# Banks, transposes and sums of a GRU gate in a fused two-layer graph network: p_n in another PSUM pool, transposes moved forward, GpSimd's sums reordered

## The chip, the cores and the metric

The kernel runs on one core of a Trainium2 chip. The metric is device time in microseconds, from the first to the last instruction. The engines are named as the profile names them: PE (TensorE, matmuls) with PEld (its weight loads), DVE (VectorE), ACT (ScalarE), POOL (GpSimd) and SP (SyncE, which here only issues DMAs).

## What is computed

The input is 64 graphs of 256 nodes with 256 features each, and a 256x256 adjacency for each. Everything is float32. Layer 0 is a normalised graph convolution with a residual and a layernorm. Layer 1 has two branches over its input x: a convolution branch along the nodes (a 1x1 convolution, ReLU, a 17-tap convolution, both with batch norm) and a message branch (a Gaussian similarity times the mask, times messages). A GRU cell joins them:

```python
x_conv = transpose(relu(h + xc))          # h: the 17-tap convolution, xc: x transposed
x_in = concatenate([x_conv, x_nmp], axis=-1)
gi = x_in @ w_ih.T + b_ih
gh = x @ w_hh.T + b_hh
r = sigmoid(gi_r + gh_r)
z = sigmoid(gi_z + gh_z)
nn_ = tanh(gi_n + r * gh_n)
x_gru = (1.0 - z) * nn_ + z * x
out = layernorm(x + x_gru)
```

## The kernel before, in words

The 64 graphs are worked in four quarters of 16 (`Q = 16`). The 17-tap convolution is done in a transformed domain, for a whole quarter at once, and so a quarter passes through stages:

- `layer0` and `layer1` of each graph (a graph's layers leave x transposed and the message branch in DRAM as `xn_d`, the layer 0 output as `x1_d`, and their transformed part in `V`);
- `products`, 12 steps of matmuls p_k with streamed weights;
- `real_transform`, `complex_begin` and `complex_end`, the inverse transform: VectorE work on the large tile `VM` (also called `M`), with no matmuls, whose `output` writes the convolution of the quarter to DRAM (`xc_d`);
- `gates`, one GRU cell (`gru`) for each graph.

Stages of different quarters are woven into each other with Python generators: each `yield` ends a piece, `merge(a, b, n)` takes a piece of b after every n of a, `take(s, n)` gives the next n pieces. The first four gates of a quarter run with the layers of the next quarter. The other twelve are `late`: 48 pieces, of which 14 go between the steps of the next quarter's `products`, and the rest are merged with `complex_end` (`end`) and, where there is a next quarter, with its first layers (`begin`). After the last quarter nothing is left to merge, so its 16 gates run alone. What stands in the code is a priority: the framework lays out each engine's instructions at build time, by that order and by what it expects to be ready. In the trace, L816 of a gate runs before L798, which stands ahead of it in the code. At run time each engine takes its instructions in the order laid out, and waits on semaphores.

There are two PSUM pools of four 128x512 tiles each. `bank` gives one of the pool `ps`, used by the layers and by the transposes p_xcT. `accbank` gives one of `psacc`, used by `products` (p_k) and by the gates (p_rz, p_n).

One gate, `gru(g)`, goes like this. It starts the loads for graph g + 1 (`load_gate`, L708 and L710). The sums r and z take 21 matmuls of 128x128 by 128x256 instead of 24, by a Strassen-like scheme over halves of the inputs; for this, GpSimd computes four sums of input halves beforehand (`input_sums`, L737 to L740, into one buffer `sums`). Each fp32 matmul is two instructions. The first twelve of the 21 (L756) fill two tiles p_rz; VectorE reads them at L769 and L770. The other nine fill two more, read at L775 and L776. ScalarE then takes two tanh (L778, L780). In the same piece come the transposes for the next graph, `transposed(g + 1)`: 4 transposes on TensorE (p_xcT, L726), and two relus on ScalarE (L728), which write the last third of the next `inputs`. Then, for each half of the nodes, 6 matmuls p_n (L793), read at L798, followed by a chain on VectorE, a tanh (L805), and after the second half the blend with x, the layernorm (with a power on GpSimd, L293, between two VectorE instructions, L292 and L301) and the output DMA.

The transposes need `xc_g`: the convolution's output loaded by `load_conv` (L704), to which `residual` (L715) adds x1 by an accumulating DMA issued by GpSimd.

Of the kernel before, what the change touches and what calls it, by code (L numbers as in the profile page):

```python
# [11 lines left out]
ALU = mybir.AluOpType  # L12
# [14 lines left out]
def kernel(  # L27
# [27 lines left out]
    nc = tc.nc  # L55
# [10 lines left out]
    Q = P // GT  # L66
# [16 lines left out]
    def accbank(name):  # L83
        return psacc.tile([P, 512], F32, tag="acc", name=name)
# [613 lines left out]


    GATE, CONV, SUMS = {}, {}, {}  # L700

    def load_conv(g):
        CONV[g] = gate.tile([P, NCH, D], F32, name="xc_g")
        nc.sync.dma_start(CONV[g], xc_d[g // Q][g % Q].rearrange("(c p) d -> p c d", p=P))  # L704
# [8 lines left out]
    def residual(g):  # L713

        nc.gpsimd.dma_start(  # L715
            CONV[g], x1_d[g // Q][g % Q].rearrange("(c p) d -> p c d", p=P), accum_op=ALU.add
        )

    def transposed(g):

        xc = CONV.pop(g)
        xcT = GATE[g][1][:, 2 * DCH :]
        p = bank("p_xcT").rearrange("p (k n) -> p k n", k=DCH)
        for k in range(DCH):
            for c in range(NCH):
                nc.tensor.transpose(p[:, k, c * P : (c + 1) * P], xc[:, c, k * P : (k + 1) * P], ident)  # L726
        for k in range(DCH):
            nc.scalar.activation(xcT[:, k], p[:, k], AF.Relu, bias=bn2_bias[:, k : k + 1])  # L728
# [5 lines left out]
    def input_sums(g):  # L734
        A11, A12, A21, A22 = halves(GATE[g][1])
        S = SUMS[g] = gate.tile([P, 4, HALF, P], F32, name="sums", bufs=1)
        nc.gpsimd.tensor_tensor(S[:, 2], A11, A21, op=ALU.subtract)  # L737
        nc.gpsimd.tensor_tensor(S[:, 0], A21, A22, op=ALU.add)  # L738
        nc.gpsimd.tensor_tensor(S[:, 1], S[:, 0], A11, op=ALU.subtract)  # L739
        nc.gpsimd.tensor_tensor(S[:, 3], A12, S[:, 1], op=ALU.subtract)  # L740

    def gru(g):

        following = g % Q + 1 < Q
        (x1, inputs), S = GATE.pop(g), SUMS.pop(g)
        trz = gate.tile([P, 4, D], F32, name="trz", bufs=1)
        nn = gate.tile([P, NCH, D], F32, name="nn", bufs=1)
        if following:  # L750
            load_gate(g + 1)
        A11, A12, A21, A22 = halves(inputs)

        def block(p, j, a, b):
            for k in range(HALF):
                nc.tensor.matmul(  # L756
                    p[:, j * D : (j + 1) * D], a[:, k], wrz[:, b, k], start=k == 0, stop=k == HALF - 1
                )

        p15, p26 = accbank("p_rz"), accbank("p_rz")  # L760
        block(p15, 0, A11, B11)
        block(p26, 0, A12, B21)
        block(p15, 1, S[:, 0], T1)
        block(p26, 1, S[:, 1], T2)
        yield
        if following:
            residual(g + 1)
        first = gate.tile([P, 2, D], F32, name="first", tag="gn")
        nc.vector.tensor_add(first, half(p15), brz_t)  # L769
        nc.vector.tensor_add(trz[:, 0:2], first[:, 0:1].to_broadcast([P, 2, D]), half(p26))  # L770
        p7, p34 = accbank("p_rz"), accbank("p_rz")
        block(p7, 0, S[:, 2], T3)
        block(p34, 0, S[:, 3], B22)
        block(p34, 1, A22, T4)
        nc.vector.tensor_add(trz[:, 3], trz[:, 1], p7[:, :D])  # L775
        nc.vector.tensor_add(trz[:, 1:3], trz[:, 1:4:2], half(p34))  # L776

        nc.scalar.activation(trz[:, 0:4:2], trz[:, 0:4:2], AF.Tanh, scale=0.5)  # L778
        nc.vector.tensor_add(trz[:, 1:4:2], trz[:, 1:4:2], first[:, 1:2].to_broadcast([P, 2, D]))
        nc.scalar.activation(trz[:, 1:4:2], trz[:, 1:4:2], AF.Tanh, scale=0.5)  # L780
        if following:
            transposed(g + 1)
        yield
        for c in range(NCH):
            terms = [(inputs[:, k, c * P : (c + 1) * P], wn[:, k]) for k in range(3 * DCH)]
            if c == 0 and following:
                input_sums(g + 1)
            if c == 1 and g % Q + 2 < Q:
                load_conv(g + 2)
            p = accbank("p_n")  # L790
            for o, part in ((1, terms[:DCH]), (0, terms[DCH:])):
                for j, (lhsT, w) in enumerate(part):
                    nc.tensor.matmul(  # L793
                        p[:, o * D : (o + 1) * D], lhsT, w, start=j == 0, stop=j == len(part) - 1
                    )

            gn = gate.tile([P, 2, D], F32, name="gn")
            nc.vector.tensor_add(gn, p.rearrange("p (i d) -> p i d", i=2), bn_t)  # L798
            nc.vector.scalar_tensor_tensor(
                gn[:, 1, :], trz[:, 2 * c], 1.0, gn[:, 1, :], op0=ALU.add, op1=ALU.mult  # L800
            )
            nc.vector.scalar_tensor_tensor(  # L802
                gn[:, 0, :], gn[:, 1, :], 0.5, gn[:, 0, :], op0=ALU.mult, op1=ALU.add
            )
            nc.scalar.activation(nn[:, c, :], gn[:, 0, :], AF.Tanh)  # L805


            if g == B - 1:
                part = slice(c, c + 1)
            elif c == NCH - 1:  # L810
                part = slice(0, NCH)
            else:
                yield
                continue
            y, t, n = x1[:, part], trz[:, 1:4:2][:, part], nn[:, part]
            nc.vector.scalar_tensor_tensor(y, t, 3.0, y, op0=ALU.add, op1=ALU.mult)  # L816
            nc.vector.scalar_tensor_tensor(n, t, 1.0, n, op0=ALU.subtract, op1=ALU.mult)
            nc.vector.tensor_sub(y, y, n)
            layernorm(y, nc.scalar, 4 * LN_EPS)
            nc.scalar.dma_start(out[g].rearrange("(c p) d -> p c d", p=P)[:, part], y)  # L820
            yield


    def merge(main, other, every=1):

        for i, _ in enumerate(main):
            yield
            if i % every == every - 1 and next(other, "end") != "end":
                yield
        yield from other  # L830

    def chain(*stages):
        for stage in stages:
            yield from stage
# [13 lines left out]
    def run(stage):  # L848
        for _ in stage:
            pass  # L850
# [69 lines left out]
    def gates(q, part):  # L920

        for i in part:
            if i == 0:
                load_conv(q * Q)
                load_gate(q * Q)
                yield
                load_conv(q * Q + 1)
                residual(q * Q)
                yield
                transposed(q * Q)  # L930
                yield
                input_sums(q * Q)
                yield
            yield from gru(q * Q + i)
# [5 lines left out]
    for q in range(NQ):  # L940
        first = (q + 1) * Q
        more = q + 1 < NQ
        end = complex_end(q)
        if more:
            if q:
                others = [both(take(late, 3 if i % 3 == 0 else 2), take(end, 2)) for i in range(AHEAD)]
            else:
                others = [nothing() for _ in range(AHEAD)]
            begin = chain(merge(layer0(first), layer0(first + 1)), graphs(first, range(AHEAD), V2, others))
        sums(0)  # L950
        real = real_transform()
        for step in range(STEPS):
            if step < 4:
                run(products(step))
            else:
                run(merge(products(step), take(real, 1)))
                run(complex_begin(step))
            if q:
                run(take(late, (0, 1, 1, 1, 1, 1, 2, 1, 2, 1, 2, 1)[step]))
            else:  # L960
                run(take(begin, 2 + step // 4))
        run(real)
        if not q:
            run(merge(begin, end, 3))
        elif more:
            run(merge(merge(take(late, 20), take(begin, 6), 3), take(end, 5), 5))
            run(begin)
        else:
            run(merge(late, end, 2))
        if more:  # L970
            run(late)
            run(end)
            for f in range(0, FL, 12):
                nc.scalar.copy(V[:, f : f + 12, :, : AHEAD * GT], V2[:, f : f + 12])
            early = gates(q, range(EARLY))
            others = [take(early, 2) for _ in range(Q)]
            run(graphs(first, range(AHEAD, Q), V, others))
            run(early)
            late = gates(q, range(EARLY, Q))
        else:  # L980
            run(gates(q, range(Q)))
# [53 lines left out]
```

## Time and profile before

The median of 3 runs is 2213.34 us (2213.03 to 2220.08). The profiled execution has a span of 2214.4 us, with 29080 instructions.

| Engine | Busy, us | Share of the span |
|---|---|---|
| PE | 2077.4 | 94% |
| PEld | 1753.5 | 79% |
| DVE | 1564.9 | 71% |
| ACT | 835.9 | 38% |
| POOL | 670.2 | 30% |

The chain that ended last is PE for 50% of the span, DVE for 13% and POOL for 5%. In that chain the gate's matmuls stand first, L756 with 18% and L793 with 9%; the three lines L738, L739 and L740 of the sums have 1% each.

How to read the lines that follow: in a group, "busy, mean ns" is followed by the idle time of the engine just before these instructions and by what ended most of it, with the line of the releaser. The idle time of a group is time in which the whole engine stood still. A line of a table of windows gives, for each engine, its busy microseconds in the stretch and the number of instructions; the last three columns are the TensorE clock granted, the share of the DMA engines, and GB/s. In the list of waits, the numbers are the total in us, the number of times and the longest. In the 40 slices of the page a slice is 2214.4 / 40 = 55.4 us long.

### The profile page before, as it was taken

To read this page: it belongs to the slowest core of one execution; us is meant where nothing else is said; L and a number is where in the kernel's file an instruction comes from. 1 tells how busy PE (TensorE), PEld (TensorE's weight loads), DVE (VectorE), ACT (ScalarE), POOL (GpSimd) and SP (SyncE) were. 2 spreads that over 40 slices of the span, in tenths; PEclk is the share of its full clock that TensorE was granted. 3 is DMA by queue.
4 is the path that set the end of the run, shared out by engine and by line. 5 is a ranking of instruction groups with operands and counts; after the bars stand their busy time and mean duration, and the time that the engine had idled before them with its cause. 6 is when DMAs were issued, how large, how long until landed. Compare 5 with 4: busy or idle time off the path is not lost.

```text
span 2214.4 us, 29080 instructions
## 1 busy us (share of the span) xinstructions
PE 2077.4 (94%) x9853; PEld 1753.5 (79%) x9853; DVE 1564.9 (71%) x3749; ACT 835.9 (38%) x1850; POOL 670.2 (30%) x653
## 2 busy tenths in 40 slices
PE   5999989969999998999999998899999999889998
PEld 4777767848888886788888887688888887678887
DVE  6655448794657899855556989955555879987666
ACT  3555533435441122446543122445554112222222
POOL 2333331113231233322322233321331123344442
PEclk9999999989999999999999999999999999999999
DMA  3655467544337644424334754433323754444342
GB/s 108 193 166 169 150 193 258 170 134 115 118 92 214 200 138 116 132 86 124 105 106 148 214 160 125 143 96 105 119 87 113 216 171 114 115 120 113 102 110 57
DMA packets 251424, 305.20 MB, mean 138 GB/s; under 512 B 18602, under 2 KB 230074, under 8 KB 251275
## 3 DMA queue, kind: packets, MB, share of 16 engines
q1 hardware_dynamic: 183180, 199.85, 29.2%
q10 hardware_dynamic: 45280, 68.04, 8.7%
q0 software_dynamic: 22816, 35.45, 8.1%
q8 instruction: 78, 1.28, 0.2%
q14 instruction: 70, 0.57, 0.1%
HBM read 200.71 MB, written 102.57 MB: 137 GB/s over the span
## 4 chain that ended last, share of the span: by engine, by line
PE 50%; DVE 13%; issue 6%; POOL 5%; ACT 4%; DMA 0%; ACTq 0%; POOLq 0%; SPq 0%; DVEq 0%
PE p_rz L756 18%; PE p_n L793 9%; PE p_k L486 8%; PE p_nmp L462 3%; PE p_out L368 2%; PE p_dft L431 2%; PE p_conv L396 2%; PE p_hT L358 2%; PE p_msg L417 1%; POOL sums L738 1%; POOL ln_rs L293 1%; PE p_dist L455 1%; POOL sums L740 1%; POOL sums L739 1%; DVE gn L798 1%
## 5 line engine op out<-in xcount | busy, mean ns | idle before, releaser
L756 PE MATMUL p_rz<-wrz,sums 128*128 128x256 f32 x1536 | 356.0, 383 | 19.5 <-DVE gn L798 9.8
L793 PE MATMUL p_n<-wn,inputs 128*128 128x256 f32 x1536 | 351.3, 381 | 16.3 <-DVE first L769 15.7
L756 PEld LDWEIGHTS p_rz<-wrz,sums 128*128 128x128 f32 x1536 | 288.6, 191 | 70.9 <-issue 15.8
L793 PEld LDWEIGHTS p_n<-wn,inputs 128*128 128x128 f32 x1536 | 285.7, 190 | 62.2 <-DVE first L769 18.9
L756 PE MATMUL p_rz<-wrz,inputs 128*128 128x256 f32 x1152 | 272.8, 380 | 2.1 <-ACT inputs L728 1.5
L293 POOL TENSOR_TENSOR ln_rs<-ln_rs,neg_half 128x2 f32<-128x2 f32 x129 | 100.4, 778 | 541.3 <-DVE ln_rs L292 455.7
L756 PEld LDWEIGHTS p_rz<-wrz,inputs 128*128 128x128 f32 x1152 | 216.8, 190 | 33.7 <-ACT inputs L728 3.6
L805 ACT ACTIVATE nn<-gn 128x256 f32<-128x256 f32 x128 | 53.2, 416 | 325.6 <-DVE gn L802 324.8
L486 PE MATMUL p_k<-u,VM 128*128 128x256 f32 x736 | 175.1, 380 | 0.8 <-DMA u<-ud 0.8
L329 POOL TENSOR_TENSOR dis<-deg,neg_half 128x2 f32<-128x2 f32 x64 | 49.9, 780 | 403.5 <-DVE deg L327 324.9
L303 ACT ACTIVATE x_g<-x_g,ln_mr,ln_rs 128x256 f32<-128x256 f32 x128 | 70.0, 593 | 256.1 <-DVE ln_mr L301 256.1
L486 PEld LDWEIGHTS p_k<-u,VM 128*128 128x128 f32 x736 | 138.3, 190 | 21.2 <-DMA u<-ud 2.2
L431 PE MATMUL p_dft<-fwd,h 128*128 128x240 f32 x512 | 118.2, 375 | 27.2 <-ACT h L400 27.2
L737 POOL TENSOR_TENSOR sums<-inputs 128x384 f32<-128x384 f32 x64 | 70.0, 1093 | 241.6 <-issue 172.0
L396 PE MATMUL p_conv<-wc,xn 128*128 128x259 f32 x512 | 128.1, 393 | 12.2 <-ACT xn L388 12.2
L358 PE MATMUL p_hT<-adjT,x 128*128 128x256 f32 x512 | 126.8, 392 | 10.0 <-DVE adjT L341 9.3
L431 PEld LDWEIGHTS p_dft<-fwd,h 128*128 128x128 f32 x512 | 95.9, 192 | 44.0 <-ACT h L400 36.4
L462 PE MATMUL p_nmp<-aT,msg 128*128 128x256 f32 x512 | 125.5, 389 | 5.0 <-DVE aT L457 5.0
L368 PE MATMUL p_out<-w,hT 128*128 128x256 f32 x512 | 124.4, 386 | 1.3 <-ACT hT L363 1.1
L396 PEld LDWEIGHTS p_conv<-wc,xn 128*128 128x128 f32 x512 | 98.0, 194 | 31.5 <-ACT xn L388 16.4
L351 POOL TENSOR_TENSOR x_t<-x_t,b_t 128x512 f32<-128x512 f32 x64 | 85.2, 1332 | 121.9 <-ACT x L350 93.2
L417 PE MATMUL p_msg<-wmsg,xn 128*128 128x256 f32 x512 | 122.0, 381 | 0.0
(153 smaller groups left out, 3880.0 us busy)
## 6 DMA issues: line engine op xcount, KB each, us to landing
u<-ud SPq DMA_DIRECT2D x284, 256.0 KB
xn_d<-xn ACTq DMA_DIRECT2D x64, 512.0 KB
inputs<-xn_d SPq DMA_DIRECT2D x64, 512.0 KB
adj_t<-in_adj_dram SPq DMA_DIRECT2D x64, 256.0 KB
x_t<-in_x_dram SPq DMA_DIRECT2D x64, 256.0 KB
x_d<-x ACTq DMA_DIRECT2D x64, 256.0 KB
x_g<-x_d SPq DMA_DIRECT2D x64, 256.0 KB
xc_d<-VM SPq DMA_DIRECT2D x64, 256.0 KB
```

The lines of the kernel that those rows point to most:

```text
L293: nc.gpsimd.tensor_tensor(rs[:, : len(chunks)], rs[:, : len(chunks)], neg_half[:, : len(chunks)], op=ALU.pow)
L303: nc.scalar.activation(y[:, c, :], y[:, c, :], AF.Identity, bias=mr[:, c : c + 1], scale=rs[:, c : c + 1])
L351: nc.gpsimd.tensor_tensor(x_t, x_t, b0_t.unsqueeze(1).to_broadcast([P, NCH, D]), op=ALU.add)
L358: nc.tensor.matmul(p[:, k, :], x1[:, mc, k * P : (k + 1) * P], adjT[:, mc, 1 - mc : 3 - mc, :].rearrange("p n q -> p (n q)"), start=mc == ...
L368: nc.tensor.matmul(p[:, c, :], hT[:, k, c * P : (c + 1) * P], w0[:, k, :], start=k == 0, stop=k == DCH - 1)
L396: nc.tensor.matmul(p, x1T[:, k, c * P : (c + 1) * P], wc1[:, k, :], start=k == 0, stop=k == DCH - 1)
L417: nc.tensor.matmul(p[:, c, :], x1T[:, k, c * P : (c + 1) * P], wmsg[:, k, :], start=k == 0, stop=k == DCH - 1)
L431: nc.tensor.matmul(p[:, t0 * FL : t1 * FL], h[:, c, k * P : (k + 1) * P], fwd[:, first : first + t1 - t0, :].rearrange("p t f -> p (t f)") ...
L462: nc.tensor.matmul(p[:, k, :], msg[:, mc, k * P : (k + 1) * P], aT[:, mc].rearrange("p n q -> p (n q)"), start=mc == 0, stop=mc == NCH - 1,)
L486: nc.tensor.matmul(p[:, j * D : (j + 1) * D], v[:, k, :], u[:, k, :], start=k == 0, stop=k == DCH - 1)
L756: nc.tensor.matmul(p[:, j * D : (j + 1) * D], a[:, k], wrz[:, b, k], start=k == 0, stop=k == HALF - 1)
L793: nc.tensor.matmul(p[:, o * D : (o + 1) * D], lhsT, w, start=j == 0, stop=j == len(part) - 1)
```

## The change

It has four parts, which keep all arithmetic as it was.

1. A flag `ALONE` is set before each quarter's `products`, from the second quarter on, and cleared where the next quarter's remaining layers begin. While it is set, the two p_n tiles of a gate come from the pool `ps` instead of `psacc`. This is meant to use the layers' banks where no layers run. (In the merged stage with `begin`, a few pieces of layers do run while it is set.)
2. `transposed(g + 1)` moves from the end of the gate's second piece to the end of the first, behind the first twelve of the 21 matmuls, and so on ScalarE ahead of the gate's two tanh.
3. For this the loads come earlier: `load_conv(g + 2)` moves from the second half of p_n to the first piece, and `residual` runs one graph further ahead: `residual(g + 2)` in the second half of p_n instead of `residual(g + 1)` after the first piece. `gates` starts the second graph's residual itself.
4. GpSimd computes the four sums in the order in which the matmuls use them: S[:, 2] comes third instead of first.

```diff
     def input_sums(g):
...
-        nc.gpsimd.tensor_tensor(S[:, 2], A11, A21, op=ALU.subtract)
         nc.gpsimd.tensor_tensor(S[:, 0], A21, A22, op=ALU.add)
         nc.gpsimd.tensor_tensor(S[:, 1], S[:, 0], A11, op=ALU.subtract)
+        nc.gpsimd.tensor_tensor(S[:, 2], A11, A21, op=ALU.subtract)
         nc.gpsimd.tensor_tensor(S[:, 3], A12, S[:, 1], op=ALU.subtract)
...
         block(p26, 1, S[:, 1], T2)
-        yield
         if following:
-            residual(g + 1)
+            transposed(g + 1)
+        if g % Q + 2 < Q:
+            load_conv(g + 2)
+        yield
...
         nc.scalar.activation(trz[:, 1:4:2], trz[:, 1:4:2], AF.Tanh, scale=0.5)
-        if following:
-            transposed(g + 1)
         yield
...
             if c == 1 and g % Q + 2 < Q:
-                load_conv(g + 2)
-            p = accbank("p_n")
+                residual(g + 2)
+            p = (bank if ALONE[0] else accbank)("p_n")
...
                 transposed(q * Q)
+                residual(q * Q + 1)
                 yield
...
+        ALONE[0] = q > 0
         sums(0)
...
             run(merge(merge(take(late, 20), take(begin, 6), 3), take(end, 5), 5))
+            ALONE[0] = False
             run(begin)
```

More of the change, by code (lines that the diff above doesn't have):

```diff
@@ L700 @@
     GATE, CONV, SUMS = {}, {}, {}
+    ALONE = [False]
     def load_conv(g):
@@ L764, in gru @@
         block(p26, 1, S[:, 1], T2)
+        if following:
+            transposed(g + 1)
+        if g % Q + 2 < Q:
+            load_conv(g + 2)
         yield
-        if following:
-            residual(g + 1)
         first = gate.tile([P, 2, D], F32, name="first", tag="gn")
@@ L780, in gru @@
         nc.scalar.activation(trz[:, 1:4:2], trz[:, 1:4:2], AF.Tanh, scale=0.5)
-        if following:
-            transposed(g + 1)
         yield
```

## The prediction

> **What bounds the kernel now.** I read the page first (share of each engine, the slices, the chain of waits), then the groups of the gate's matmuls, then a table of windows by stage, then who waited for whom in the one long stretch where TensorE has gaps, and last the chain in order of time where that stretch ends. The page:
>
> ```profile
> PE 2077.4 (94%) x9853; PEld 1753.5 (79%) x9853; DVE 1564.9 (71%) x3749; ACT 835.9 (38%) x1850; POOL 670.2 (30%) x653
> ...
> PE   5999989969999998999999998899999999889998
> ...
> DVE  6655448794657899855556989955555879987666
> ...
> L756 PE MATMUL p_rz<-wrz,sums 128*128 128x256 f32 x1536 | 356.0, 383 | 19.5 <-DVE gn L798 9.8
> L793 PE MATMUL p_n<-wn,inputs 128*128 128x256 f32 x1536 | 351.3, 381 | 16.3 <-DVE first L769 15.7
> ...
> L756 PE MATMUL p_rz<-wrz,inputs 128*128 128x256 f32 x1152 | 272.8, 380 | 2.1 <-ACT inputs L728 1.5
> ```
>
> TensorE is the engine in demand, but not evenly: it dips in three places, and there VectorE stands at 8 to 9 tenths. In front of the gate's matmuls TensorE sat idle 19.5 + 16.3 + 2.1 = 37.9 us, nearly all for VectorE reading a PSUM bank (L798, L769) or for GpSimd's sums. The table of windows gives busy time by stage (columns: PE, PEld, DVE, ACT, POOL with counts, granted clock, DMA share, GB/s):
>
> ```profile
> 700.00:780.00 80.00, 80.00 (x376) 70.42 (x376) 68.25 (x134) 13.70 (x28) 17.72 (x15) 1.00 0.68 204
> 800.00:900.00 100.00, 85.66 (x383) 71.38 (x381) 97.57 (x223) 27.86 (x59) 40.26 (x34) 0.95 0.43 121
> ...
> 1320.00:1420.00 100.00, 84.34 (x383) 69.58 (x382) 97.57 (x223) 28.41 (x60) 39.96 (x34) 0.97 0.43 121
> ...
> 1820.00:1955.00 135.00, 119.41 (x549) 100.24 (x548) 131.37 (x270) 29.77 (x60) 49.89 (x44) 1.00 0.38 108
> 1955.00:1975.00 20.00, 17.39 (x78) 13.67 (x77) 16.05 (x29) 4.75 (x10) 9.12 (x9) 1.00 0.60 167
> 1975.00:2200.00 225.00, 225.00 (x1073) 198.13 (x1072) 158.24 (x309) 58.12 (x122) 94.55 (x91) 1.00 0.39 101
> ```
>
> While `products` runs (700 to 780) and in the 15 last gates (1975 to 2200) TensorE has no gap at all: nothing is to be had there. All of TensorE's gaps in gates lie in the three stretches where the gates of the quarter before run against `complex_end`, and in those VectorE is busy 97.57 of 100, 97.57 of 100 and 131.37 of 135 us. **So the gate's PSUM waits are mostly a symptom: VectorE is the bound there.** The list of waits from 1820 to 1975 shows which ones:
>
> ```profile
> PE p_n L793 <- DVE first L769: 7.2, 8, 1.3
> ...
> PE p_rz L756 <- DVE gn L798: 6.7, 7, 1.3
> ...
> PE p_rz L756 <- POOL sums L738: 2.9, 4, 1.6
> ```
>
> And the chain of waits in order of time at the hand-over from this stretch to the last gates (g = 48 is the first that needs the `complex_end` just finished):
>
> ```profile
> 1953.72 3.02 DMA xc_d<-VM
> ...
> 1957.78 3.83 DMA xc_g<-xc_d
> ...
> 1973.08 6.86 PE p_rz L756 x30
> ```
>
> **What the Trainium skill says.** "PSUM — Partial Sum Buffer", Specifications: eight banks of 2 KiB a partition, and Terms: a matmul's output stays within one. The two pools hold four 128x512 fp32 tiles each, all eight; moving p_n takes a bank from the layers' four, it makes none. The trace agrees only indirectly (p_n waits for L769, which frees a bank). "GPSIMD Engine Reference", Key points: GpSimd shares its SBUF interfaces with VectorE and they contend when VectorE has two SBUF inputs. The trace agrees: L301 has a mean of 842 ns from 1820 to 1955, where the first of the sums (L737) runs beside it, and took 0.16 us at 2109.15, alone. "TensorE: Matmul & The Clock Gate", What's actually happening: after an idle window the array runs at half clock. The trace agrees: before p_conv at 888.13 TensorE idled 3.92 us, and the window 880 to 900 has a clock of 0.83.
>
> **The change part by part.** No instruction is added or removed: 64 gates keep 42 + 24 gate matmul instructions (in the chain 9.06 and 5.18 us), a transpose group (0.44 us), two relus (0.47 us each), four sums (1.0 to 1.3 us each), two loads. Per gate TensorE needs 9.06 + 5.18 + 0.44 = 14.68 us before and after. Only orders and banks move.
>
> (1) p_n out of the gate's banks, from the second quarter's `products` on. Before, six tiles a gate rotate over four banks: p_n of half 0 needs L769 to have read p_rz's first tile, of which the last matmul stands 24 instructions and the transposes earlier: 24 x 0.216 + 0.44 = 5.6 us. That is how far VectorE may lag before TensorE stops. After, four tiles rotate over four banks; the next gate's first tile needs L769 48 instructions and a transpose group back: 48 x 0.216 + 0.44 = 10.8 us. TensorE may lead by 5.2 us more. Where VectorE doesn't lag this is worth nothing. Where it is the bound (three stretches), it saves no VectorE time; it moves TensorE's work ahead once per stretch.
>
> (2) Transposes and relus ahead of the tanh. Before, L728 queues on ScalarE behind the tanh of the gate's own sums (L778, L780), which wait for VectorE; the sums then wait for L728 (L738: 27.5 us from 1820 to 1975) and the next gate's matmuls for the sums (2.9 us). After, the relus hang on TensorE's first 24 instructions and, at most, on the layernorm of the gate before. Queued behind the transposes on TensorE are the other 18 gate instructions: they wait if xc is late. The accumulating DMA lands in 5.1 us (page). The transposes move ahead by 18 instructions (3.9 us), the load and the residual by about half a gate (some 7 us), so I cost this at nothing: hidden by the gate before (14.68 us).
>
> (3) Order of the sums. S[:, 0] and S[:, 1] no longer stand behind S[:, 2]. S[:, 2] does not need the relu and ran in its shadow, so the order alone gives about 0 (bounds: 0 to 1.0 us a gate, the length of L737, only where the sums are late).
>
> Now the sums. First and second stretch: TensorE's waits of gates in the part with the moved bank (at 818.86, 834.07, 849.33: 1.86 + 1.72 + 2.66 = 6.2 us) turn into a lead, but soon the next quarter's layers come, whose matmuls need results of VectorE in its queue order, and the lead is lost again. Bounds 0 and 6.2; I take VectorE's own idle time, 100 - 97.57 = 2.4 us each, 4.8 together. Third stretch: VectorE idles 135 - 131.37 = 3.6 us, of which 3.1 is L301 waiting for GpSimd's power, which stays; so `complex_end` ends as before, at 1953.7. Then the chain needs 3.0 + 3.8 us of DMA and a residual issued at 1960.06 that takes 5.1 us, so gate 48 can't begin before 1965.2; its transposes began at 1968.46, behind the gates before. A lead of 5.2 us fills that: 1968.46 - 1965.2 = 3.3 us, and about 1 of the 1.5 us that TensorE waits after it for relu and sums. Together 4.3 us. Total 4.8 + 4.3 = 9.1 us: **2213.3 - 9.1 = 2204 us.**
>
> **The rivals.** *Nothing moves (2212).* VectorE is the bound in all three stretches, gates keep 18.4 us there (p_rz starts at 1914.77, 1933.22, 1951.58), and TensorE merely waits elsewhere. For it: 97% in the table. Against: after the third stretch TensorE has its own gaps. *The waits were TensorE's own (2192).* If VectorE's order lets gates go first and `complex_end` later, under layers where VectorE is only 62% busy (61.82 of 100 from 900 to 1000), the waits vanish: all 37.9 us would give 2175; half, since layers pin the lead, 2213 - 20 = about 2193, and a slow-clock spell less (at 849 to 853 eight gaps of 0.21): 2192. *The hand-over comes bare (2223).* Gate work that TensorE makes ready sooner goes ahead of `complex_end` in VectorE's order. In the third stretch that order matters: VectorE still has some 13 us of gate work after 1953.7 (16.05 us busy from 1955 to 1975, less what belongs to gate 48). If that all goes first, `complex_end` ends at 1967, gate 48 begins 11.5 us later, at 1978 instead of 1968.5: 10 us lost, with TensorE idle as no layers are left to fill it. The two merged stages where p_n now takes layers' banks point the same way.
>
> **How the numbers follow.** 2204 has 0.47, nothing 0.17, the larger gain 0.20, slower 0.16. 0.3% is 6.6 us: faster is below 2206.7. About seven tenths of the first case lie there (0.34), the larger gain (0.20) and a little of "nothing" (0.02): 0.56. Slower is the third rival and 0.02: 0.18. The rest, 0.26, is the same. The range goes from a little beyond the middle of the larger gain to short of the worst hand-over: 2190 to 2220.
>
> **What would show it.** Right: idle time before p_n with releaser L769 near zero from 1820 to 1955, VectorE still at 97% there, `complex_end`'s last output within 2 us of 1953.7, gate 48's transposes near 1965, and no new gap from 1975 on. Wrong: `complex_end` ending later against the gates (third rival), fewer than 97% of VectorE with shorter gates (second), or transposes waiting for xc_g's DMA, which I took as hidden.

## The result, and the profile after

The changed kernel takes 2234.15 us (median of four runs, 2231.58 to 2236.54); the kernel before takes 2213.26 us beside it. The ratio is 1.0087, with a 95% interval of 1.0063 to 1.0110: **slower by 0.9%**, some 19 us, where 2204 us and a gain had been forecast. The profiled execution, with a span of 2229.8 us, is the shortest of the four.

In the changed kernel the lines are shifted by one to four: the sums S[:, 0], S[:, 1], S[:, 2], S[:, 3] are L738 to L741, the residual is L716, the transposes L727, the relus L729, the gate's matmuls L757 and L794, the reads of p_rz L772, L773, L778 and L779. `output`, the last part of `complex_end`, keeps its line, L664.

From the page of the changed kernel (busy time, the groups of the gate's matmuls):

```profile
PE 2085.3 (94%) x9853; PEld 1760.2 (79%) x9853; DVE 1602.1 (72%) x3749; ACT 841.9 (38%) x1850; POOL 662.6 (30%) x653
...
L757 PE MATMUL p_rz<-wrz,sums 128*128 128x256 f32 x1536 | 362.3, 384 | 15.1 <-POOL sums L738 10.5
L794 PE MATMUL p_n<-wn,inputs 128*128 128x256 f32 x1536 | 353.7, 384 | 6.8 <-DVE first L772 6.8
...
L757 PE MATMUL p_rz<-wrz,inputs 128*128 128x256 f32 x1152 | 274.7, 382 | 8.6 <-DVE first L772 5.7
```

Two things are to be seen. The idle time before p_n fell from 16.3 to 6.8 us, as forecast: the moved bank does what it is for. (What is left, 3.9 and 2.9 us, lies in the first two stretches.) And VectorE's busy time rose from 1564.9 to 1602.1 us **with the same 3749 instructions**. No instruction was added to it, so the same ones took 37.2 us longer.

The table of windows of the changed kernel (columns as before the change: us, then busy time and number of instructions of PE, PEld, DVE, ACT and POOL, granted clock, DMA share, GB/s):

```profile
800.00:900.00 100.00, 83.19 (x362) 70.26 (x362) 96.37 (x214) 27.23 (x56) 33.88 (x31) 0.90 0.41 116
...
1820.00:1955.00 135.00, 120.71 (x547) 100.54 (x546) 127.44 (x244) 27.41 (x57) 41.84 (x40) 0.99 0.36 102
...
1990.00:2200.00 210.00, 210.00 (x1004) 184.97 (x1003) 159.55 (x289) 57.84 (x116) 91.85 (x86) 1.00 0.41 104
```

VectorE is nearly as full as before in these windows (96.37 of 100 us, 127.44 of 135), but gets less done: 214 instructions in 100 us where it was 223, 244 in 135 us where it was 270. At the end TensorE has no gap in either kernel; the gates 49 to 63 take 219.8 us in both. The windows are the same times, but not quite the same work. To put the loss in its place, I cut the run at points that both kernels have: the last p_k matmul of a quarter, the last output (L664) of its `complex_end`, the end of gate 48's p_n.

| Piece, us | before | after |
|---|---|---|
| first stretch, last p_k to last output | 130.4 | 135.0 |
| second stretch | 130.4 | 134.4 |
| third stretch | 133.9 | 143.7 |
| hand-over, last output to the end of gate 48's p_n | 31.9 | 33.3 |
| gates 49 to 63 | 219.8 | 219.8 |

The three stretches and the hand-over make 4.6 + 4.0 + 9.8 + 1.4 = 19.8 us: that is the loss. (The two spans differ by 15.4 us only: in this run the first p_k came 2.5 us earlier, and the first quarter was 3.0 us shorter. Ahead of the first p_k the work is the same in all kernels, and it comes between 320.7 and 326.4 us in the runs below.)

The third stretch holds the same 269 VectorE instructions in both kernels, so its window can be compared directly. Before, and then after:

```profile
1819.40:1953.70 134.30, 118.98 (x548) 100.20 (x547) 130.57 (x269) 29.45 (x60) 48.67 (x43) 1.00 0.38 108
```

```profile
1823.60:1967.70 144.10, 126.65 (x569) 104.42 (x568) 139.53 (x269) 28.34 (x58) 45.54 (x44) 0.99 0.35 99
```

The stretch is 9.8 us longer, and VectorE's busy time in it 139.53 - 130.57 = 9.0 us. Its groups, before and after (busy us, mean ns), show which instructions grew: those of `complex_end`, each of which has two inputs in SBUF.

```profile
L664 DVE SCALAR_TENSOR_TENSOR VM<-turn,VM 128x256 f32<-128x256 f32 x32 | 13.7, 441 | 0.0
L564 DVE SCALAR_TENSOR_TENSOR turn<-VM 128x256 f32<-128x256 f32 x23 | 11.4, 514 | 0.0
```

```profile
L664 DVE SCALAR_TENSOR_TENSOR VM<-turn,VM 128x256 f32<-128x256 f32 x32 | 18.6, 601 | 0.0
L564 DVE SCALAR_TENSOR_TENSOR turn<-VM 128x256 f32<-128x256 f32 x23 | 14.3, 625 | 0.0
```

(The layernorm's L301, which the prediction had seen held, is the exception: five of its seven take 0.16 us now; in the gate shown below the residual L716 stands on GpSimd between the power and the first sum.) The timeline (start, duration) of one gate shows when they grow. First the kernel before, GpSimd and then VectorE; `x2` marks two instructions in a row:

```profile
1911.31 0.71 POOL L293 TENSOR_TENSOR ln_rs<-ln_rs,neg_half 128x2 f32<-128x2 f32 x1 [8.55 <-DVE ln_rs L292]
1912.01 0.99 POOL L737 TENSOR_TENSOR sums<-inputs 128x384 f32<-128x384 f32 x1
1916.74 2.30 POOL L738 TENSOR_TENSOR sums<-inputs 128x384 f32<-128x384 f32 x1 [3.73 <-ACT inputs L728]
1919.11 1.06 POOL L739 TENSOR_TENSOR sums<-sums,inputs 128x384 f32<-128x384 f32 x1
1920.25 1.06 POOL L740 TENSOR_TENSOR sums<-inputs,sums 128x384 f32<-128x384 f32 x1
...
1913.95 0.74 DVE L664 SCALAR_TENSOR_TENSOR VM<-turn,VM 128x256 f32<-128x256 f32 x2
...
1920.37 1.22 DVE L664 SCALAR_TENSOR_TENSOR VM<-turn,VM 128x256 f32<-128x256 f32 x1
```

And a gate of the changed kernel:

```profile
1881.31 0.71 POOL L293 TENSOR_TENSOR ln_rs<-ln_rs,neg_half 128x2 f32<-128x2 f32 x1 [12.72 <-DVE ln_rs L292]
1881.99 1.22 POOL L716 DMA_DIRECT2D xc_g<-x_d  x1
1882.78 1.46 POOL L738 TENSOR_TENSOR sums<-inputs 128x384 f32<-128x384 f32 x1
1883.73 1.46 POOL L740 TENSOR_TENSOR sums<-inputs 128x384 f32<-128x384 f32 x1
1884.68 1.45 POOL L739 TENSOR_TENSOR sums<-sums,inputs 128x384 f32<-128x384 f32 x1
1886.21 1.07 POOL L741 TENSOR_TENSOR sums<-inputs,sums 128x384 f32<-128x384 f32 x1
...
1882.14 5.42 DVE L664 SCALAR_TENSOR_TENSOR VM<-turn,VM 128x256 f32<-128x256 f32 x2
```

Before, the first sum ran behind the layernorm's power, and the rest had to wait for the relu: a 128x256 instruction beside one of the later sums was held for about its length (1.22 us instead of 0.41). After, the relu is long done, the sums run in one block behind the power, and the two outputs that had just been issued get through only at the block's end: 5.42 us where two take 0.74. Taken singly, the first of the two lasts 4.28 us, over three sums that start 0.95 us apart; the other lasts 1.21 us, beside the fourth, which starts 1.53 us after the third. (GpSimd's spans are rough in this profile: the first of the two starts 0.64 us ahead of the first sum by it, so where exactly the hold begins is not shown.) The laid-out order on GpSimd shows in it too: S[:, 2] (L740) stands between S[:, 0] and S[:, 1], although the code has it third.

The list of PE's waits in that stretch (us in total, times, longest) confirms the bank and shows what came instead:

```profile
PE p_rz L757 <- POOL sums L738: 7.8, 5, 2.3
PE p_rz L757 <- DVE first L772: 5.7, 6, 1.3
```

No wait of p_n for the reader of p_rz is left in this stretch (before: 7.2 us for L769). But p_rz waits for that reader now, and more for the sums. The chain in order of time at the hand-over answers to the one shown of before:

```profile
1972.52 3.71 DMA xc_g<-xc_d
...
1976.75 0.07 POOL xc_g L716
...
1977.50 1.21 POOL ln_rs L293
...
1978.74 0.96 DVE ln_mr L301
...
1985.28 0.02 ACT nn L806
...
1985.60 0.47 ACT inputs L729
```

The load of the convolution in this chain begins at 1972.52 instead of 1957.78, because the last output came 14.0 us later (it ends at 1967.7 instead of 1953.7). What follows it is not only TensorE's: the second of two residuals (gate 49's) waits on GpSimd for this load, a layernorm's power (L293) stands behind it in GpSimd's queue, VectorE's work of gate 47 behind the power, then gate 47's tanh (L806), and in ScalarE's queue behind the tanh the relu that gate 48's matmuls need. In the kernel before the chain runs the same way (L715, L293 at 1962.92, L301 at 1964.15), and in both the tanh starts 8.5 us after that residual. In the changed kernel TensorE's timeline has two gaps there, of 4.63 and 2.92 us:

```profile
1979.20 1.09 PE L727 MATMUL p_xcT<-ident,xc_g 128*128 128x128 f32 x4 [4.63 <-DMA xc_g<-x_d]
...
1986.11 2.08 PE L757 MATMUL p_rz<-wrz,inputs 128*128 128x256 f32 x4 [2.92 <-ACT inputs L729]
```

### The profile page after: what moved, and what is told of

Its sections match the earlier page's. It is cut to its first block, busy times and chain, and to the rows that moved or that the text cites. A ratio compares the mean times of both kernels' runs of the same rounds, so it can differ in the third digit from the quotient of the medians.

```text
span 2229.8 us, 29161 instructions
## 1 busy us (share of the span) xinstructions
PE 2085.3 (94%) x9853; PEld 1760.2 (79%) x9853; DVE 1602.1 (72%) x3749; ACT 841.9 (38%) x1850; POOL 662.6 (30%) x653
## 4 chain that ended last, share of the span: by engine, by line
PE 55%; DVE 10%; issue 8%; POOL 3%; ACT 2%; DMA 1%; SPq 0%; POOLq 0%; ACTq 0%; DVEq 0%
PE p_rz L757 19%; PE p_n L794 10%; PE p_k L486 8%; PE p_nmp L462 3%; PE p_out L368 3%; PE p_dft L431 3%; PE p_hT L358 2%; PE p_conv L396 2%; PE p_msg L417 2%; DVE VM L664 1%; PE p_dist L455 1%; PE p_xcT L727 1%; DVE gn L803 1%; POOL ln_rs L293 1%; PE p_x1T L387 1%
## 5 line engine op out<-in xcount | busy, mean ns | idle before, releaser
L757 PE MATMUL p_rz<-wrz,sums 128*128 128x256 f32 x1536 | 362.3, 384 | 15.1 <-POOL sums L738 10.5
L794 PE MATMUL p_n<-wn,inputs 128*128 128x256 f32 x1536 | 353.7, 384 | 6.8 <-DVE first L772 6.8
L757 PEld LDWEIGHTS p_rz<-wrz,sums 128*128 128x128 f32 x1536 | 289.0, 192 | 63.8 <-POOL sums L738 13.5
L794 PEld LDWEIGHTS p_n<-wn,inputs 128*128 128x128 f32 x1536 | 291.0, 192 | 52.3 <-DVE first L772 7.3
L293 POOL TENSOR_TENSOR ln_rs<-ln_rs,neg_half 128x2 f32<-128x2 f32 x129 | 97.7, 757 | 647.1 <-DVE ln_rs L292 552.9
L757 PE MATMUL p_rz<-wrz,inputs 128*128 128x256 f32 x1152 | 274.7, 382 | 8.6 <-DVE first L772 5.7
L757 PEld LDWEIGHTS p_rz<-wrz,inputs 128*128 128x128 f32 x1152 | 217.8, 191 | 41.7 <-DVE first L772 8.1
L806 ACT ACTIVATE nn<-gn 128x256 f32<-128x256 f32 x128 | 53.3, 417 | 287.0 <-DVE gn L803 286.7
L368 PE MATMUL p_out<-w,hT 128*128 128x256 f32 x512 | 128.0, 394 | 14.0 <-DVE gn L799 12.4
L716 POOL DMA_DIRECT2D xc_g<-x_d x64 | 78.6, 1235 | 179.9 <-DMA xc_g<-xc_d 143.1
L368 PEld LDWEIGHTS p_out<-w,hT 128*128 128x128 f32 x512 | 99.1, 196 | 33.4 <-DVE gn L799 12.8
L457 DVE TENSOR_TENSOR aT<-aT,adjT 128x512 f32<-128x512 f32 x64 | 46.6, 728 | 105.4 <-ACT aT L456 105.2
```

The lines of the kernel that those rows point to most:

```text
L293: nc.gpsimd.tensor_tensor(rs[:, : len(chunks)], rs[:, : len(chunks)], neg_half[:, : len(chunks)], op=ALU.pow)
L368: nc.tensor.matmul(p[:, c, :], hT[:, k, c * P : (c + 1) * P], w0[:, k, :], start=k == 0, stop=k == DCH - 1)
L716: nc.gpsimd.dma_start(CONV[g], x1_d[g // Q][g % Q].rearrange("(c p) d -> p c d", p=P), accum_op=ALU.add)
L757: nc.tensor.matmul(p[:, j * D : (j + 1) * D], a[:, k], wrz[:, b, k], start=k == 0, stop=k == HALF - 1)
L794: nc.tensor.matmul(p[:, o * D : (o + 1) * D], lhsT, w, start=j == 0, stop=j == len(part) - 1)
```

## The experiments

Three theories were to be told apart. **P, the port:** the early relus let GpSimd's sums run as one block, and VectorE's instructions with two inputs in SBUF are held meanwhile. "GPSIMD Engine Reference", Key points, of the Trainium skill names the contention with two SBUF inputs; how long one is held is read from the traces here. **K, the banks:** p_n in the layers' banks makes layers or gates wait, and VectorE's order suffers. **R, the loads:** the earlier loads and residuals get in the way. The kernel before, run beside them, had medians of 2213 to 2217 us.

**e1: only the banks moved** (the kernel before with the flag).

```diff
-            p = accbank("p_n")
+            p = (bank if ALONE[0] else accbank)("p_n")
...
+        ALONE[0] = q > 0
         sums(0)
...
+            ALONE[0] = False
             run(begin)
```

> The kernel before with the first part alone: p_n in the layers' banks while the flag is set; transposes, loads and sums as before. Theory K (banks: a p_n tile that VectorE reads late holds a bank that a layer's matmul needs): p_out waits 6 us in each of the two merged stages, as in the changed kernel, while the last quarter gains 2 to 4 us from TensorE's longer lead, in all 2216 to 2224. Theory P (port: the four sums run as one block and keep VectorE out): the sums are as before, so VectorE's busy time stays near 1565 us, complex_end's last output of the last quarter stays near 1953 us, and the time is within 3 us of 2213 or below. Theory R (the early loads and residuals do it): as P.

Measured: 2217.3 us beside 2216.96 for the kernel before, ratio 1.0003 (0.9994 to 1.0012). The three stretches are the 130.4, 130.4 and 133.9 us of before, and VectorE's busy time is 1566.2 us. The waits of p_out that K had expected are not there. K falls as the cause, and so does any gain of the banks alone. The list of PE's waits in its third stretch shows why there is none:

```profile
PE p_rz L757 <- ACT inputs L729: 8.1, 6, 2.2
PE p_rz L757 <- POOL sums L739: 2.9, 3, 1.7
```

The waits of p_n are gone; TensorE comes earlier to the next gate and waits there for the relus, which still stand behind the tanh.

**e2: only the transposes and the loads moved** (the old order of the sums, p_n in the gates' banks).

```diff
         block(p26, 1, S[:, 1], T2)
-        yield
         if following:
-            residual(g + 1)
+            transposed(g + 1)
+        if g % Q + 2 < Q:
+            load_conv(g + 2)
+        yield
...
-        if following:
-            transposed(g + 1)
         yield
...
             if c == 1 and g % Q + 2 < Q:
-                load_conv(g + 2)
+                residual(g + 2)
...
                 transposed(q * Q)
+                residual(q * Q + 1)
```

> The kernel before with the transposes and the loads moved, p_n in the gates' own banks, the sums in the old order of the code. P: the relus come early, so the first two sums run together, but the third and fourth still wait for the one before, and VectorE gets in between: half of the extra collisions, VectorE busy 1570 to 1585 us, time 2210 to 2220. K: no bank of the layers is held, no wait of p_out over 1 us, time 2213 or less. R (a residual stands ahead of the sums in GpSimd's queue and waits for its load): the loss is here, 2225 or more.

Measured: 2228.0 us, ratio 1.0050 (1.0031 to 1.0069); VectorE's busy time is 1591.7 us, 26.8 more than before, at the same count. The stretches are 134.8, 134.9 and 141.7 us. Its third window, and the timeline of one gate (GpSimd, then VectorE):

```profile
1826.50:1968.50 142.00, 121.57 (x545) 103.34 (x544) 137.48 (x269) 28.31 (x58) 46.31 (x44) 0.96 0.36 101
```

```profile
1884.03 1.47 POOL L738 TENSOR_TENSOR sums<-inputs 128x384 f32<-128x384 f32 x1
1884.98 1.46 POOL L739 TENSOR_TENSOR sums<-inputs 128x384 f32<-128x384 f32 x1
1886.52 1.07 POOL L740 TENSOR_TENSOR sums<-sums,inputs 128x384 f32<-128x384 f32 x1
1887.66 1.05 POOL L741 TENSOR_TENSOR sums<-inputs,sums 128x384 f32<-128x384 f32 x1
...
1883.39 4.47 DVE L664 SCALAR_TENSOR_TENSOR VM<-turn,VM 128x256 f32<-128x256 f32 x2
1887.79 1.21 DVE L566 SCALAR_TENSOR_TENSOR turn<-VM 128x256 f32<-128x256 f32 x1
```

So this part alone makes the stretches longer, in the third by VectorE instructions held beside GpSimd's block: 6.9 of its 7.8 us are VectorE's busy time. Here the first of the two outputs lasts 3.34 us, over the two sums that start 0.95 us apart, the second 1.21 us beside the third sum, and L566 1.21 us beside the fourth. The loss is larger than P had foretold (1570 to 1585 us of VectorE, 2210 to 2220), and the time alone fits R (2225 or more); the next run tells the two apart.

**e8: of e2 only the loads and residuals**, with the transposes at their old place.

```diff
         block(p26, 1, S[:, 1], T2)
+        if g % Q + 2 < Q:
+            load_conv(g + 2)
         yield
-        if following:
-            residual(g + 1)
...
-                load_conv(g + 2)
+                residual(g + 2)
...
+                residual(q * Q + 1)
```

> The kernel before with the loads and residuals moved as in the change, but the transposes at their old place, p_n in the gates' banks and the sums in the old order. P: the relus come as late as before, so the sums run apart as before; VectorE's loss in the last stretch stays near 20.6 us; 2213 to 2217, no difference from before of over 0.2%. R: the loss of the run with transposes and loads moved (0.5%) shows here too, 2222 or more.

Measured: 2215.5 us beside 2215.34, ratio 1.0000 (0.9991 to 1.0009), third stretch 134.3 us in the window, as before. R falls. What is left of e2 is the place of the transposes, and with it of the relus.

**e3: only the order of the sums.**

```diff
-        nc.gpsimd.tensor_tensor(S[:, 2], A11, A21, op=ALU.subtract)
         nc.gpsimd.tensor_tensor(S[:, 0], A21, A22, op=ALU.add)
         nc.gpsimd.tensor_tensor(S[:, 1], S[:, 0], A11, op=ALU.subtract)
+        nc.gpsimd.tensor_tensor(S[:, 2], A11, A21, op=ALU.subtract)
```

> The kernel before with GpSimd's new order of the sums alone. P: S[:, 2] no longer runs apart beside the layernorm but fills the gap between S[:, 0] and S[:, 1], so that three sums run without a break and hold up VectorE; VectorE busy 1580 us or more, 2219 to 2228, and complex_end of the last quarter ends 4 to 8 us later. K and R: no effect, 2213 within 3 us.

Measured: 2216.1 us, ratio 0.9993 (0.9985 to 1.0002). Nothing moved, because the order on the engine did not: S[:, 2] doesn't need the relu, and the build still lays it out first. What P had foretold of this run missed for that reason.

**e4: the change, with the banks moved in the last quarter alone.**

```diff
-        ALONE[0] = q > 0
+        ALONE[0] = q == NQ - 1
```

> The changed kernel with p_n in the layers' banks in the last quarter only, where no layers run; in the two merged stages p_n is in the gates' banks again. K: the two waits of p_out (6.35 us and a slow clock after each) go, and the time falls by 10 to 15 us to 2219 to 2224. P: those waits only show VectorE's backlog, which stays; the last quarter is unchanged; 2230 to 2236, at most 5 us gained.

Measured: 2234.94 us, ratio 1.0085 (1.0069 to 1.0101). In the changed kernel two matmuls of the layers (p_out) wait for a bank, 6.2 us each in the list of waits; here these two waits are gone, and the stretches stay at 134.4, 134.3 and 143.6 us. A long wait of the engine in demand that costs nothing: VectorE was the bound behind it.

**e5: the change, with S[:, 2] kept out of the space between S[:, 0] and S[:, 1]** by computing it from S[:, 1], which is the same sum but for rounding.

```diff
-        nc.gpsimd.tensor_tensor(S[:, 2], A11, A21, op=ALU.subtract)
+        nc.gpsimd.tensor_tensor(S[:, 2], A22, S[:, 1], op=ALU.subtract)
```

> The changed kernel with one operand of one sum changed: S[:, 2] = A22 - S[:, 1], which is the same number as A11 - A21, but must wait for S[:, 1]. So the four sums take the same time on GpSimd, but S[:, 2] can't fill the gap between S[:, 0] and S[:, 1]. Theory P (the sums run without a break and keep VectorE out): the time VectorE loses in its two-input instructions in the last stretch falls from 29 us to 24 to 27, complex_end's last output comes 2 to 6 us earlier, time 2226 to 2232. Theory R (early loads, and a residual ahead of the sums in GpSimd's queue): unchanged, 2234 within 3 us.

Measured: 2231.64 us, ratio 1.0081 (1.0066 to 1.0096); VectorE's busy time is 1587.8 us, 14.3 less than in the changed kernel; the third stretch is 141.4 us instead of 143.7, much as in e2 (141.7). The filled space makes the block denser, and that is worth 2 us in this stretch. The whole time is not told from that of the changed kernel, as the intervals overlap, and it lies in P's range and in R's.

**e6 and e7: the change, and the kernel before, without the sums.** Both leave out GpSimd's four sums of every gate; the matmuls read a fixed tile in their place, so these kernels leave out a part of the computation and serve for times alone. The edit of e7 (e6 has the same):

```diff
-        S = SUMS[g] = gate.tile([P, 4, HALF, P], F32, name="sums", bufs=1)
-        nc.gpsimd.tensor_tensor(S[:, 2], A11, A21, op=ALU.subtract)
-        nc.gpsimd.tensor_tensor(S[:, 0], A21, A22, op=ALU.add)
-        nc.gpsimd.tensor_tensor(S[:, 1], S[:, 0], A11, op=ALU.subtract)
-        nc.gpsimd.tensor_tensor(S[:, 3], A12, S[:, 1], op=ALU.subtract)
+        SUMS[g] = FIXED[0]
```

> The changed kernel without GpSimd's sums: the four sums of inputs are left out, and the gates' matmuls read a tile that is filled once. All else is as in the changed kernel. P: VectorE loses almost nothing in the three stretches (20 + 20 + 29 us before), which then last 116 to 121 us or as long as TensorE needs; the time is 2175 to 2200, and within 5 us of the kernel before without sums, since what set the two apart is gone. R: the two kernels without sums still stand 10 to 20 us apart.

> The kernel before without GpSimd's sums (left out in the same way, the gates' matmuls read a tile that is filled once). P: 2175 to 2200, within 5 us of the changed kernel without sums. R: 10 to 20 us faster than that one.

Measured: e6 2159.11 us, ratio 0.9751 (0.9736 to 0.9765); e7 2151.97 us, ratio 0.9721 (0.9706 to 0.9735). The pages' lines of busy time, e6 and then e7:

```profile
PE 2064.8 (96%) x9853; PEld 1756.2 (81%) x9853; DVE 1468.9 (68%) x3750; ACT 843.7 (39%) x1850; POOL 373.4 (17%) x397
```

```profile
PE 2064.1 (96%) x9853; PEld 1755.7 (82%) x9853; DVE 1470.3 (68%) x3750; ACT 836.9 (39%) x1850; POOL 372.9 (17%) x397
```

Both are faster than P had foretold (2175 to 2200), and they stand 7 us apart, more than P's 5 and less than R's 10. VectorE does the same work in 1469 and 1470 us, one memset more included. So the sums on GpSimd make its instructions last 1564.9 - 1470.3 = 94.6 us longer in all in the kernel before, and 1602.1 - 1468.9 = 133.2 us in the changed one. And of the loss of 0.87%, 0.9751 - 0.9721 = 0.30% (some 7 us) stays without the sums. By this difference some 12 of the 19 us are the sums'. They are not spread evenly. The first stretch, e7 and then e6:

```profile
778.90:893.10 114.20, 111.02 (x530) 96.80 (x529) 109.25 (x288) 36.16 (x78) 17.53 (x18) 0.99 0.52 149
```

```profile
774.80:891.50 116.70, 112.43 (x534) 97.52 (x534) 109.94 (x289) 36.56 (x79) 17.40 (x18) 0.99 0.50 147
```

Cut as in the table above, the stretches are 113.9, 113.8 and 114.2 us in e7 and 116.3, 117.1 and 114.6 us in e6. So without the sums the change still costs 2.4 and 3.3 us in the first two stretches, and 0.4 us in the third. Of the 9.8 us of the third stretch nearly all are the sums', but of the 4.6 and 4.0 us of the first two more than half are not. (The split is rough in the third stretch, where TensorE has hardly a gap once the sums are gone: it is busy for 113.9 of 114.2 us in e7 and for all of it in e6.)

**e11 and e12: the 7 us without sums, split.** To e7, which leaves the sums out, e11 adds e2's edit, e12 that of e1.

> Without GpSimd's sums (left out, the matmuls read a tile filled once), and of the change the transposes and loads alone, with p_n in the gates' own banks. It tells where the 7 us come from that stay without sums (2159 against 2152). If the transposes cost them: 2157 to 2161. If p_n in the layers' banks does: 2150 to 2154.

> Without GpSimd's sums (left out in the same way), and of the change p_n in the layers' banks alone. If the banks cost the 7 us that stay without sums: 2157 to 2161. If the transposes do: 2150 to 2154, or some us below, from TensorE's longer lead.

Measured: 2155.88 and 2155.28 us, ratios 0.9727 (0.9713 to 0.9742) and 0.9722 (0.9708 to 0.9737). Both times lie between the two ranges expected. By the ratios neither is told from e7, and e11 is not told from e6 either. The traces say more, by one profile each. I take the piece from the second quarter's first p_k to the end; it leaves out the first quarter, in which e7's profiled execution, the slowest of its four, took 345.0 us from its first p_k to the next quarter's, and the other three 339.2 to 340.9. The piece repeats well: 1541.3 us before, 1541.6 in e3 and 1541.0 in e8. Without sums it is 1484.2 us in e7, 1485.4 in e12, 1489.0 in e11 and 1492.9 in e6. So of 8.7 us the transposes and loads alone bring 4.8, the banks alone 1.2, and 2.7 come only with both.

The part of the transposes lies mostly in the first two stretches: 116.3 and 115.7 us in e11 instead of 113.9 and 113.8. VectorE stands idle there 1.2 to 2.5 us longer in e11 and e6 than in e7, and has one instruction more ahead of the last output, a read of a gate's p_rz. What brings this about was not tried.

The hand-over is 30.5 us in e7, 31.8 in e12, 32.0 in e11 and 34.3 in e6. In e6 TensorE waits 5.1 us there for a relu (L730 in its lines), and its chain of waits is the one seen before:

```profile
1899.51 5.15 DMA xc_g<-xc_d
...
1905.52 1.18 POOL xc_g L717
1906.70 0.76 POOL ln_rs L293
...
1913.22 0.02 ACT nn L803
...
1913.54 0.47 ACT inputs L730
```

The order of tanh and relu is as old as the kernel: before, the tanh stands ahead of the relu as well, and TensorE waits for the relu 0.7 us. In all four runs the tanh starts 7.7 us after gate 49's residual on GpSimd, and that residual starts 10.7 us after the last output in e6 and 8.7 us after it in e7. So 2.0 of the 3.8 us are a load that landed later; whether by chance or by the change, one profile of each does not tell.

**e9 and e10: the sums on VectorE**, in the kernel before (e9) and in the changed one (e10).

```diff
-        nc.gpsimd.tensor_tensor(S[:, 2], A11, A21, op=ALU.subtract)
-        nc.gpsimd.tensor_tensor(S[:, 0], A21, A22, op=ALU.add)
-        nc.gpsimd.tensor_tensor(S[:, 1], S[:, 0], A11, op=ALU.subtract)
-        nc.gpsimd.tensor_tensor(S[:, 3], A12, S[:, 1], op=ALU.subtract)
+        nc.vector.tensor_tensor(S[:, 2], A11, A21, op=ALU.subtract)
+        nc.vector.tensor_tensor(S[:, 0], A21, A22, op=ALU.add)
+        nc.vector.tensor_tensor(S[:, 1], S[:, 0], A11, op=ALU.subtract)
+        nc.vector.tensor_tensor(S[:, 3], A12, S[:, 1], op=ALU.subtract)
```

> The kernel before with the four sums on VectorE instead of GpSimd. P: VectorE adds four instructions of some 0.53 us a gate (three quarters of L818's 0.69 us) in place of the 2.6 to 2.75 us that it loses a gate to GpSimd's sums; a stretch shortens by 3 to 6 us, 2195 to 2208, if TensorE does not wait for sums that stand in VectorE's backlog. R (GpSimd's queue was the trouble, not VectorE): VectorE gets 2.1 us a gate more to do and the time rises by 10 us or more.

> The changed kernel with the four sums on VectorE instead of GpSimd. P: no collisions, so the same stretches as in the kernel before with sums on VectorE, within 7 us of it (the rest that stayed without sums), 2200 to 2215, and 20 us or more faster than the changed kernel. R: slower than the changed kernel.

Measured: e9 2196.75 us, ratio 0.9912 (0.9895 to 0.9928), **faster than both kernels**; e10 2203.8 us, ratio 0.9944 (0.9930 to 0.9959), some 30 us faster than the changed kernel. From e9's page:

```profile
PE 2072.7 (94%) x9853; PEld 1760.4 (80%) x9853; DVE 1584.6 (72%) x4005; ACT 838.4 (38%) x1850; POOL 372.9 (17%) x397
...
L740 DVE TENSOR_TENSOR sums<-inputs,sums 128x384 f32<-128x384 f32 x64 | 36.4, 569 | 0.4
```

VectorE takes 569 ns for a sum (L740) for which GpSimd takes 1187 ns on the mean in the kernel before; "GPSIMD Engine Reference", Key points, says that for elementwise work VectorE is about twice as fast, and this agrees. The 256 sums add 1584.6 - 1470.3 = 114.3 us to VectorE, some 20 us more than the 94.6 us that it lost to the same sums on GpSimd. The place of the gain was not the expected one: the stretches are longer (139.5, 140.6, 144.2 us), since VectorE's order now has more gate work ahead of the last output (337 instructions in the third instead of 269, 33 of them sums). In return, gate 47's p_n ends 11.8 us before that output instead of 15.0 us after it. From first p_k to first p_k the middle quarters gain 12.4 and 9.3 us (507.3 and 508.6 instead of 519.7 and 517.9); the last, with no layers to fill in, loses 6.3 to its last p_n (500.6 instead of 494.3), and its PE waits around the hand-over show the bare one:

```profile
PE p_xcT L726 <- DMA xc_g<-x_d: 9.8, 2, 9.0
PE p_rz L756 <- DVE sums L737: 9.6, 1, 9.6
```

Between e9 and e10 lie 0.9944 - 0.9912 = 0.32%. That the rest of the change costs 0.3% with the sums off GpSimd is thus seen twice, here and in e6 against e7.

## Why the prediction was wrong, point by point

- **What bounds the kernel: right.** VectorE is the bound in the three stretches, and TensorE's gaps there are symptoms. The experiments bear it out: banks alone (e1) change nothing, two waits of 6.2 us come and go for nothing (e4), and what shortens the stretches is less time of VectorE (e7).
- **(1) The lead of 5.2 us: there, but worth nothing.** p_n's waits for the reader of p_rz vanished from the third stretch, and gate 47's p_n ends 6.9 us after the last output instead of 15.0. In the first two stretches the 2.4 us each were not had: e1 gives 0 there. (The bound of 6.2 us beside it is a little high: the trace has idle times of 1.70, 1.56 and 2.50 us at the three places, 5.8 in all.) At the hand-over the 4.3 us were not had either, and here a path was missing in the sum. The prediction let gate 48 begin when its own load and residual were done and TensorE was free. But its relu stands behind gate 47's tanh, and that goes back over VectorE and GpSimd's queue to gate 49's load, in the kernel before as well, where the relu starts 17.3 us after the last output. TensorE's lead can't move that; it became two gaps of 4.63 and 2.92 us (in e1, one of 4.13 for the relu, with a hand-over of 34.0 us instead of 31.9).
- **(2) Transposes and relus "at nothing": the step that failed.** The loads and residuals are hidden, as worked out (e8: 1.0000). But the late relu had also held GpSimd back. It kept the sums apart, and the prediction asked only whether the sums would come late, not beside what they would run once early. It had the contention in hand, with a number: L301 took 842 ns beside the first sum and 0.16 us alone. It took that as something that stays as it is. From that came "so `complex_end` ends as before, at 1953.7". It ended at 1967.7: 4.2 us of the difference were there at the start of the stretch, 9.8 us came in it, and 9.0 of these are VectorE's busy time. Apart from the sums the move is not quite hidden either: 2.4 and 1.9 us of the first two stretches come with the transposes when the sums are left out (e11), for a reason that stays open.
- **(3) The order of the sums: about right** alone (0 predicted, 0.9993), but not in the way given: S[:, 2] doesn't wait for the relu and so stays first on the engine, whatever the code says, and the run did not try the term. Behind early relus S[:, 2] fills the space between S[:, 0] and S[:, 1], which e5 puts at 2 us in the third stretch.
- **The rivals.** "The hand-over comes bare" had 1967 for `complex_end`'s end and 1978 for gate 48, and 1967.7 and 1979.2 came. But its mechanism, gate work that goes ahead in VectorE's order, is not what the trace shows: the last output stands behind the same work in both orders, 47 reads of p_rz's first tile and 46 gates' reads of p_n. The times were hit by chance, through another cause. Its mechanism does occur, in e9. "The waits were TensorE's own" falls with e1. "Nothing moves" had VectorE as the bound, and e1, e3 and e8 are that case; it too let VectorE's work stay as it was.
- **The size.** In the place of -9.1 us stand some +12 us from sums that hold VectorE, most of them in the third stretch, and some +7 us that stay without sums. In e6's trace these stand mainly in the first two stretches (2.4 and 3.3 us) and in the hand-over (3.8, of which 2.0 are one load). The transposes alone bring most of the former (e11); why they do is open. The range ended at 2220, short of the third rival, and no term of it let VectorE's own instructions grow.

## What to carry to other kernels

Before moving work of one engine earlier, ask not only who waits for it but beside what it will then run: a wait can be what keeps two engines apart that hold each other up. Compare busy time at equal instruction counts, and the means of the same group, in two traces; if they differ, the same instructions took longer, here because another engine held them, and the busy share of that engine is no measure of its work. Where GpSimd does elementwise work beside a VectorE that is the bound, try it on VectorE: here it took half the time for each and gave 0.9%.

## What the runs showed of the hardware

- A VectorE instruction with two inputs in SBUF can be held over several GpSimd instructions, when these follow each other without a gap: 5.42 us for two 128x256 instructions beside four sums, 4.47 us beside three (e2), against 0.74 us alone. In the gates shown a single instruction lasted 4.28 us, over three sums that start 0.95 us apart, and 3.34 us over two of them (e2). Beside a single sum it was held about as long as that sum ran (1.22 us beside 1.06).
- GpSimd's sums cost VectorE 94.6 us of holding in the kernel before, for the 256 of them some 0.37 us each, and 133.2 us (0.52 us each) when they run in blocks. I had taken the loss as one of L301 alone.
- Leaving these sums out gains 2.8% (e7), though GpSimd is busy for only 30% of the span.
